# A sandwich of attention and feed-forward blocks: a stretch of products moved, a norm moved to VectorE, and the ending split over two banks

## The chip, the cores and the metric

The kernel runs on one core of one Trainium2 chip. The core has five engines that run their own instruction streams in order: TensorE (PE in the profile, its weight loads PEld), VectorE (DVE), ScalarE (ACT), GpSimd (POOL), and SyncE (SP), which here issues the DMAs. They wait for each other by semaphores. The metric is the device time of one execution in microseconds (us). Before the change it is 620.03 us, the median of 3 runs (619.95 to 620.16).

## The reference

The input x is 2 batches of 512 tokens with 256 features, in float32. Four blocks follow each other, each with a norm before and a norm after it:

```python
x = x + layernorm(L0_attn(layernorm(x)))   # 16 heads of 128, RoPE, causal softmax
x = x + layernorm(L0_ffn(layernorm(x)))    # 2048 wide, gelu(gate) * up, 4-bit weights with scales
x = x + layernorm(L1_attn(layernorm(x)))   # linear attention, running sums along the tokens
x = x + layernorm(L1_ffn(layernorm(x)))    # 688 wide, silu(gate) * up, weights looked up in a table of 16
```

The linear attention has phi(x) = elu(x) + 1 on q and k, the running sums of k and of k*v along the tokens, q*sum(k*v) / (q*sum(k) + eps), and an output product. All products are float32.

## The kernel before

The 1024 tokens are cut into units of 256 tokens (u = 0 to 3, two per batch), and a unit into two tiles of 128 tokens. NT is 4 tiles per batch, HT is 2 tiles per unit, NK is 2 chunks of 128 features.

*Start.* The four tiles of the first batch are loaded, `statistics`, `variance` and `factor` make mean and 1/deviation for each tile, and ScalarE subtracts the mean. For the first two tiles the transposed, normalised x comes out of a product with a diagonal matrix that holds 1/deviation (`diagonal(t)`, tile `wu`); that product is PE's first real work, after 18 warm-up products on constants. ScalarE writes the first two tiles through `spread(t)`, an access pattern that permutes the columns while it goes.

*First attention.* The 32 pairs of batch and head run as slots, `slot(i)` with i up to NS + 1 (NS = 32). In one slot head i's scores are made and softmaxed, head i-1's probabilities are turned and multiplied with the values (`attended(i - 1)`, `ps_t<-pT,v`), and head i-2 is projected out (`projected_out(i - 2)`). `turned_p(i)` writes four DVE transposes and the four DMAs that finish the transposed probabilities (`pT<-turned`). In the last slots the pairs of gate and up products of the first FFN unit (`main`, which is `ffn_hidden(0)`) fill PE; each `next(main)` is one product, `ps_mm<-xT,wg` or `ps_s<-xT,wu`. ScalarE makes gelu (`ge<-ps_mm`), VectorE the product with up (`hT<-ge,ps_s`), which frees the banks.

*Feed-forwards and second attention.* `ffn_hidden(u)` and `ffn_out(u)` run for the four units in turn, then `silu_hidden(u)` and `silu_out(u)`. Among their products the planner puts the rest: `linear_attention(u)`, with its projections (`ps_mm<-xT,wqkv_sb`, `ps_s<-xT,wqkv_sb`), exponentials, running sums, reciprocals and output product (`wout_sb,lT`). `norms(u, y, stage, to)` makes the norm after a block and the one ahead of the next: statistics on DVE, the power for 1/deviation on POOL, the normalised tile `ln` on ACT, its 32x32 transposes on DVE (`tr<-ln`), and four DMAs that put the blocks in place (`xT<-tr`). For the third norm of the last unit alone it goes another way: ACT writes `ln` through a permuting access pattern, PE makes four transposes (`ps_t<-ident,ln`, line 288), and ACT copies the result out.

*Order.* The order of all instructions is fixed when the program is written. A planner (`Times`, `Engine`, lines 109 to 183) keeps a clock per engine with a cost for each instruction. Each chain of small work is a generator that yields the time to wait, for example `yield until(lT)`; `poll()`, called after each product, writes the steps of the chains that are due by that clock. So a chain's step that becomes due earlier lands ahead of a later product. Engines then run their own streams in this order. Every instruction of DVE, ACT and POOL has line 183 in the profile, every DMA line 165, every product line 281.

*Banks.* Products write PSUM banks under four names, mm, s, t and o, with two banks each. A product that wants a bank waits until the reader of the one before last has finished.

*Halved products.* `halved[0]` makes `matmul` write each product as two of 64 columns of weights instead of one of 128. It is on from the attention on, and `norms` turns it off at the third norm of the last unit.

*The end.* `silu_out(3)` makes the last tile's product in two halves of 128 columns in one bank. Then `written` takes the statistics of each half (`st_last`), joins them, takes 1/deviation on POOL, subtracts the mean, multiplies and adds to x, and writes the tile out.

Of the kernel before, what the change touches and what calls it, by code (L numbers as in the profile page):

```python
# [10 lines left out]
F32 = mybir.dt.float32  # L11
# [5 lines left out]
AF = mybir.ActivationFunctionType  # L17
ALU = mybir.AluOpType

P = 128  # L20
# [13 lines left out]
HT = 2  # L34
# [156 lines left out]
def sandwich_kernel(  # L191
    ctx: ExitStack,
    tc: tile.TileContext,
    x: bass.AP,
    wq: bass.AP,
    wk: bass.AP,
# [98 lines left out]


    x0 = [const.tile([P, NT, D], F32, name=f"x0_{b}") for b in range(B)]
    cols_sb = const.tile([P, 3 * NH + 2 * NK], F32, name="cols_sb")
    for t in range(NT):
        sync.dma_start(out=x0[0][:, t, :], in_=x[0][t * P : (t + 1) * P, :])  # L300
    sync.dma_start(out=cols_sb, in_=cols)
# [51 lines left out]
    def add_scaled(x, y, rstd):  # L353

        vector.scalar_tensor_tensor(x, y, rstd, x, ALU.mult, ALU.add)

    def norms(u, y, stage, to, eps=EPS, strided=False):
# [13 lines left out]
        by_blocks = (u, stage) != (NUNIT - 1, 3)  # L371
        for j in range(HT):
            rstd, shift = second[j]
            yield until(rstd, shift)
            to_n, from_x = n[:, j, :], x[j]
            if not by_blocks:
                to_n = to_n.rearrange("p (k f c) -> p k f c", k=NK, c=4)
                from_x = from_x.rearrange(
                    "p (c f k) -> p k f c" if strided else "p (k c f) -> p k f c", k=NK, c=4
                )  # L380
            elif strided:
# [4 lines left out]
        if by_blocks:  # L386

            tr = acts.tile([P, 4, NK, HT, 32], F32, tag="ln", name=f"tr{stage}_{u}")
            for j in range(HT):
                vector.transpose(  # L390
                    tr[:, :, :, j, :], n[:, j, :].rearrange("p (k c f) -> p c k f", k=NK, c=4)
                )
            for a in range(4):
                sync.dma_start(
                    out=to[:, a].rearrange("p k j t -> p (k j t)"),
                    in_=tr[32 * a : 32 * a + 32].rearrange("f c k j t -> f c (k j t)"),
                )
        else:

            halved[0] = False  # L400
            pt = bank("t")
            for kc in range(NK):
                for j in range(HT):
                    transpose(
                        pt[:, kc * TU + j * P : kc * TU + (j + 1) * P],
                        n[:, j, kc * P : (kc + 1) * P],
                    )
            for kc in range(NK):
                scalar.copy(
                    to[:, :, kc].rearrange("p a j t -> p j a t"),  # L410
                    pt[:, kc * TU : (kc + 1) * TU].rearrange("p (j a t) -> p j a t", j=HT, a=4),
                )
# [97 lines left out]
    with ExitStack() as at:  # L510
# [69 lines left out]
        def first_norms(b, wait):  # L580
# [104 lines left out]
            else:  # L685
# [13 lines left out]
                for t in range(NT):  # L699
                    statistics(t)  # L700
                    variance(t)
                    if t < HT:
                        scalar.activation(*spread(t), AF.Identity, bias=mv[:, t, 0:1], scale=-1.0)
                    factor(t)
# [28 lines left out]
            for kc in range(NK):  # L733
# [5 lines left out]
                )  # L739
            yield 30.0  # L740
            while holder[0] is not None:
# [362 lines left out]
        def slot(i):  # L1104
# [96 lines left out]
            if i in (1, 2):  # L1201

                ahead = projection("q", i + 2)
                next(ahead)
            if 1 <= i < NS + 1:
                attended(i - 1)
# [8 lines left out]
            if i < NS - HG:  # L1215
                if i > 1:
                    values(i // 2 + 1, odd)
            elif i <= NS:
                next(main)
                next(main)  # L1220
# [58 lines left out]
    def linear_attention(u):  # L1279
# [63 lines left out]
        for ch in range(NK):  # L1343
            for t in range(HT):
# [3 lines left out]
                yield 0.3  # L1348
        yield until(lT)
        po = bank("t" if last else "o")  # L1350
# [11 lines left out]

        yield from norms(u, [po[:, j * D : (j + 1) * D] for j in range(HT)], 3, t, 16 * EPS)
        xT3[u] = t
# [8 lines left out]
    def silu_hidden(u):  # L1373
# [12 lines left out]
        for o in range(0, NO, 2):  # L1386
# [22 lines left out]
            yield  # L1409

    def silu_out(u):
        for t in range(HT):
            po = bank("o")[:, :D]
            last = (u, t) == (NUNIT - 1, HT - 1)
            for cs in [slice(0, P), slice(P, D)] if last else [slice(0, D)]:
                for o in range(NO):
                    matmul(
                        po[:, cs],
                        hT2[u % 2][:, o, t * P : (t + 1) * P],
                        wd[:, o, cs],  # L1420
                        o == 0,
                        o == NO - 1,
                    )
                    if o % 2 and (o + 1 < NO or cs.stop < D):
                        yield
            begin(written(u, t, po))
            yield

    def written(u, j, y):
# [10 lines left out]

        st = small.tile([P, 2, 6], F32, tag="st", name="st_last")
        mv = small.tile([P, 2], F32, tag="mv", name="mv_last")
        for c in range(2):
            vector.bn_stats(st[:, c, :], y[:, c * P : (c + 1) * P])
        vector.bn_aggr(mv, st)
        ve = small.tile([P, 1], F32, tag="ve", name="ve_last")
# [3 lines left out]
        centred = acts.tile([P, HT, D], F32, tag="ln", name="centred")[:, 0, :]  # L1450
        vector.tensor_scalar(centred, y, mv[:, 0:1], None, ALU.subtract)
        add_scaled(x, centred, rstd)
# [28 lines left out]
def _layout(i):  # L1481
# [21 lines left out]
    def turned(w):  # L1503
        return w.reshape(4, 32, -1).transpose(1, 0, 2).reshape(w.shape)

    def by_half(s):
        return s.reshape(4, 2, -1).transpose(1, 0, 2).reshape(s.shape)
# [12 lines left out]
    named = {  # L1520
        "x": i[a0 + "h"],
        "wq": by_head_chunk(i[a0 + "wq"]),
        "wk": by_head_chunk(i[a0 + "wk"]),
# [43 lines left out]
```

## Time and profile before

| | |
|---|---|
| median of 3 runs | 620.03 us (619.95 to 620.16) |
| the profiled execution | 620.06 us |
| its span in the profile | 618.1 us, so 1.96 us lie outside it |
| instructions | 13150 |
| PE busy | 611.0 us, 99% of the span |
| DVE busy | 483.3 us, 78% |
| ACT busy | 312.0 us, 50% |
| POOL busy | 275.9 us, 45% |
| TensorE clock granted | full in all 40 slices |

All times of a trace count from the start of the span. In a row of the timeline the first number is the start, the second the length of a run of like instructions (their number after the x), then engine, line, operation, tile written and tiles read. What stands in brackets at the end is how long the engine was idle before it, and what ended the idle time. In a row of groups the columns are line, engine, operation, tiles, shapes and count, then busy time and mean of one in ns, then idle time ahead.

### The profile page before, as it was taken

What the parts mean: (1) busy time and instruction counts of PE and PEld (TensorE: products, weight loads), DVE (VectorE), ACT (ScalarE), POOL (GpSimd) and SP (SyncE); (2) the same over time, 40 slices, a digit from 0 to 9 for tenths busy, and PEclk for the clock granted to TensorE, in tenths of its full rate; (3) what the DMA queues carried; (4) which work ended last, traced back from release to release, by engine and by line L of the source; (5) the groups of instructions that cost most, each with busy time, mean ns of one, the idle gap of its engine ahead of it and who ended that gap; (6) DMA issues with size and microseconds to landing.
All of it is one profiled execution on the core that took longest, in us unless ns stands there. A gap on an engine that the chain in (4) does not pass through costs nothing.

```text
span 618.1 us, 13150 instructions
## 1 busy us (share of the span) xinstructions
PE 611.0 (99%) x4876; PEld 397.7 (64%) x4876; DVE 483.3 (78%) x1159; ACT 312.0 (50%) x717; POOL 275.9 (45%) x353
## 2 busy tenths in 40 slices
PE   8999999999999999999999999999999999999996
PEld 6555655555555555656667788888666666666676
DVE  6989989887887999989899989779985463384853
ACT  5657776776666657667566741234123313425130
POOL 5355656454553575755667300440360160163341
PEclk9999999999999999999999999999999999999999
DMA  8467474755547547556543521310000001001000
GB/s 227 137 168 211 107 198 125 173 165 147 155 125 182 164 113 190 156 143 173 124 130 63 131 57 24 113 35 18 1 20 19 1 1 35 1 5 31 27 27 18
DMA packets 43599, 60.90 MB, mean 99 GB/s; under 512 B 5136, under 2 KB 31504, under 8 KB 43536
## 3 DMA queue, kind: packets, MB, share of 16 engines
q1 hardware_dynamic: 43536, 60.07, 37.5%
q8 instruction: 39, 0.64, 0.4%
q14 instruction: 24, 0.20, 0.1%
HBM read 28.33 MB, written 1.05 MB: 48 GB/s over the span
## 4 chain that ended last, share of the span: by engine, by line
PE 96%; DVE 2%; issue 1%; DMA 0%; POOL 0%; ACT 0%; POOLq 0%; DVEq 0%
PE ps_mm L281 39%; PE ps_o L281 22%; PE ps_s L281 21%; PE ps_t L281 14%; DVE rr L183 0%; DMA x<-in_x 0%; DVE turned L183 0%; DVE st L183 0%; DVE wu L183 0%; DVE xTv L183 0%; DVE xT L183 0%; DVE ra L183 0%; DVE hT L183 0%; POOLq L1563 0%; PE ps_t L288 0%
## 5 line engine op out<-in xcount | busy, mean ns | idle before, releaser
L183 DVE SCALAR_TENSOR_TENSOR rr<-ps_mm,cols_sb,sin_sb 64x512 f32<-64x512 f32 (+1 forms) x126 | 93.4, 741 | 3.7 <-PE ps_mm L281 0.8
L183 POOL TENSOR_TENSOR wg<-wg,scratch 128x752 f32<-128x752 f32 x30 | 53.8, 1794 | 91.0 <-DVE scratch L183 88.7
L281 PE MATMUL ps_mm<-xT,wg 128*64 128x256 f32 (+2 forms) x680 | 85.8, 379 | 0.0
L183 ACT ACTIVATE p<-p,mn 128x512 f32<-128x512 f32 (+3 forms) x128 | 70.3, 551 | 28.1 <-DVE mn L183 27.9
L281 PE MATMUL ps_s<-xT,wu 128*64 128x256 f32 (+1 forms) x652 | 82.0, 379 | 0.0
L281 PE MATMUL ps_o<-wd,hT 128*64 128x256 f32 (+2 forms) x676 | 78.3, 375 | 0.0
L281 PE MATMUL ps_t<-pT,v 128*64 128x256 f32 (+3 forms) x512 | 75.1, 433 | 0.0
L281 PEld LDWEIGHTS ps_mm<-xT,wg 128*64 128x64 f32 (+2 forms) x680 | 56.5, 139 | 19.1 <-ACT ge L183 0.3
L281 PEld LDWEIGHTS ps_o<-wd,hT 128*64 128x64 f32 (+1 forms) x676 | 55.5, 141 | 20.7
L183 ACT ACTIVATE p<-p,rs 128x512 f32<-128x512 f32 (+3 forms) x128 | 61.4, 551 | 11.4 <-DVE rs L183 9.8
L281 PEld LDWEIGHTS ps_s<-xT,wu 128*64 128x64 f32 (+1 forms) x652 | 54.4, 139 | 18.1 <-DVE hT L183 0.3
L281 PEld LDWEIGHTS ps_t<-pT,v 128*64 128x64 f32 x512 | 42.0, 137 | 34.8 <-issue 25.5
L281 PE MATMUL ps_o<-wo,oT 128*64 128x256 f32 x512 | 61.4, 379 | 0.0
L281 PE MATMUL ps_mm<-xT,wq 128*64 128x512 f32 (+2 forms) x252 | 59.4, 582 | 0.4 <-ACT xT L183 0.4
L281 PE MATMUL ps_mm<-xT,wk 128*64 128x512 f32 x248 | 59.1, 592 | 0.0
L281 PEld LDWEIGHTS ps_o<-wo,oT 128*64 128x64 f32 x512 | 42.5, 137 | 25.2 <-issue 15.1
L183 POOL TENSOR_TENSOR ra<-ra,cos_sb 128x512 f32<-128x512 f32 (+1 forms) x33 | 41.1, 1246 | 39.3 <-ACT ra L183 37.1
L281 PE MATMUL ps_s<-kT,qT 128*64 128x64 f32 (+5 forms) x384 | 57.4, 425 | 0.1
L183 DVE STREAM_TRANSPOSE turned<-p 128x512 f32<-128x512 f32 (+3 forms) x128 | 54.1, 479 | 2.1 <-DMA pT<-turned 0.6
L281 PE MATMUL ps_mm<-wv,xTv 128*64 128x256 f32 x464 | 55.6, 379 | 0.0
L183 DVE TENSOR_TENSOR hT<-ge,ps_s 128x512 f32<-128x512 f32 x32 | 21.8, 684 | 41.6 <-ACT ge L183 22.9
L281 PEld LDWEIGHTS ps_s<-kT,qT 128*64 128x64 f32 x384 | 34.3, 137 | 24.2 <-issue 7.5
(157 smaller groups left out, 933.6 us busy)
## 6 DMA issues: line engine op xcount, KB each, us to landing
pT<-turned SPq DMA_DIRECT2D x128, 208.0 KB, 3.9
wo<-in_wo SPq DMA_DIRECT2D x17, 256.0 KB, 4.1
wv<-in_wv SPq DMA_DIRECT2D x16, 256.0 KB, 4.0
wq<-in_wq SPq DMA_DIRECT2D x15, 256.0 KB, 4.4
wk<-in_wk SPq DMA_DIRECT2D x15, 256.0 KB, 4.0
xT<-tr SPq DMA_DIRECT2D x44, 64.0 KB, 2.1
pk_g<-in_gate_p SPq DMA_DIRECT2D x4, 256.0 KB, 4.3
sc_g<-in_gate_s SPq DMA_DIRECT2D x8, 128.0 KB, 4.1
```

What stands on the lines that cost most here:

```text
L183: return write(*args, **more)
L281: nc.tensor.matmul(out[part], lhsT=lhsT[:, part], rhs=rhs, start=start, stop=stop, **more)
```

## The change

It has five parts.

1. The first two tiles of x are loaded from a second copy of the input, `x_turned`, whose columns are permuted on the host. ScalarE then writes the normalised tiles without `spread`. The two tiles are loaded again in the plain order, from the plain input, 20 us of the planner's clock later, for the residual.
2. In slot NS - 2 the two `next(main)` that stood after `turned_p` stand ahead of `attended(i - 1)`, so head 29's values come after the FFN's pair of products.
3. The last unit's output product of the linear attention is due 0.8 us of the planner's clock earlier. With this and the other parts the planner places several steps differently. The projections of the linear attention: unit 0's one gate/up pair later among the products of `ffn_hidden(1)`, those of units 1 and 2 one pair earlier, unit 3's after 20 of the 24 halved products of `silu_out(0)` instead of after 8. The output products: unit 0's after all eight blocks of `ffn_out(1)` instead of within the seventh, unit 1's after six blocks of `ffn_out(2)` instead of seven, unit 2's after seven blocks of `ffn_out(3)` instead of after that and a pair of `silu_hidden(0)`, unit 3's after all 24 halved products of `silu_out(1)` instead of 20.
4. `last_norms` takes the place of `norms` for the third norm of the last unit. VectorE subtracts and multiplies in one instruction per tile and makes the transposes, and four DMAs put the blocks in place. PE's transposes, ACT's `ln` and the copies are gone, and `halved[0]` stays on to the end.
5. In `silu_out(2)` the first two of six row blocks are taken for both tiles, then the other four for both. In `silu_out(3)` the two halves of the last tile go to two banks, o and t, and the statistics of the first half stand ahead of the second half's products. The subtraction of the mean is two instructions of 128 columns instead of one.

```diff
     for t in range(NT):
-        sync.dma_start(out=x0[0][:, t, :], in_=x[0][t * P : (t + 1) * P, :])
+        src = x_turned if t < HT else x[0]
+        sync.dma_start(out=x0[0][:, t, :], in_=src[t * P : (t + 1) * P, :])
...
+    def last_norms(u, y, to, eps):
+        x = [xs[u][:, j, :] for j in range(HT)]
+        def factors(y, eps):
...
+            vector.bn_stats(st, y)
+            vector.bn_aggr(mv, st)
+            ve = small.tile([P, 1], F32, tag="ve", name="ve")
+            vector.tensor_scalar(ve, mv[:, 1:2], eps, None, ALU.add)
+            rstd = small.tile([P, 1], F32, tag="rstd", name="rstd")
+            pool.tensor_tensor(rstd, ve, mhalf[:, :1], ALU.pow)
+            return mv, rstd
+        first = [factors(t, eps) for t in y]
+        second = []
+        for j in range(HT):
+            add_scaled(x[j], y[j], first[j][1])
+            second.append(factors(x[j], EPS))
+        yield 1.0
...
+        for j in range(HT):
+            mv, rstd = second[j]
+            vector.tensor_scalar(n[:, j, :], x[j], mv[:, 0:1], rstd, ALU.subtract, ALU.mult)
+            turned_about(tr, n, j)
+        brought(to, tr)
+        yield 1.0
+        for j in range(HT):
+            mv, rstd = first[j]
+            shift = small.tile([P, 1], F32, tag="shift", name="shift")
+            pool.tensor_scalar(shift, mv[:, 0:1], rstd, -1.0, ALU.mult, ALU.mult)
+            scalar.activation(x[j], x[j], AF.Identity, bias=shift)
+        yield until(to)
...
-        else:
-            halved[0] = False
-            pt = bank("t")
-            for kc in range(NK):
-                for j in range(HT):
-                    transpose(
...
                     if t < HT:
-                        scalar.activation(*spread(t), AF.Identity, bias=mv[:, t, 0:1], scale=-1.0)
+                        scalar.activation(
+                            n[0][:, t, :],
+                            x0[b][:, t, :],
+                            AF.Identity,
+                            bias=mv[:, t, 0:1],
+                            scale=-1.0,
+                        )
...
-            yield 30.0
+            yield 20.0
+            if b == 0:
+                for t in range(HT):
+                    sync.dma_start(out=x0[b][:, t, :], in_=x_rows[b][t * P : (t + 1) * P, :])
+            yield 10.0
...
+            if i == NS - 2:
+                next(main)
+                next(main)
             if 1 <= i < NS + 1:
                 attended(i - 1)
...
-            elif i <= NS:
+            elif NS - 2 < i <= NS:
                 next(main)
                 next(main)
...
-        yield until(lT)
+        yield until(lT) - 0.8 * last
...
-        yield from norms(u, [po[:, j * D : (j + 1) * D] for j in range(HT)], 3, t, 16 * EPS)
+        y = [po[:, j * D : (j + 1) * D] for j in range(HT)]
+        yield from last_norms(u, y, t, 16 * EPS) if last else norms(u, y, 3, t, 16 * EPS)
...
     def silu_out(u):
+        halves = [slice(0, P), slice(P, D)]
+        if u == NUNIT - 2:
+            parts = [(t, slice(0, D), os) for os in (range(NO - 4), range(NO - 4, NO)) for t in range(HT)]
+        else:
+            parts = [(0, slice(0, D), range(NO))]
+            parts += [(1, cs, range(NO)) for cs in (halves if u == NUNIT - 1 else [slice(0, D)])]
+        po = {}
+        for n, (t, cs, os) in enumerate(parts):
+            if (t, cs.start) not in po:
+                po[t, cs.start] = bank("t" if cs.start else "o")[:, :D]
...
+            if cs.stop - cs.start < D:
+                if not last_st:
+                    last_st.append(small.tile([P, 2, 6], F32, tag="st", name="st_last"))
+                vector.bn_stats(last_st[0][:, len(last_po), :], po[t, cs.start][:, :P])
+                last_po.append(po[t, cs.start][:, :P])
...
-        vector.tensor_scalar(centred, y, mv[:, 0:1], None, ALU.subtract)
+        for c in range(2):
+            cs = slice(c * P, (c + 1) * P)
+            vector.tensor_scalar(centred[:, cs], last_po[c], mv[:, 0:1], None, ALU.subtract)
```

More of the change, by code (lines that the diff above doesn't have):

```diff
@@ L194, in sandwich_kernel @@
     x: bass.AP,
+    x_turned: bass.AP,
     wq: bass.AP,
@@ L294, in until @@
         return max(0.0, times.written(*aps) - now[0])
+    x_rows = x
     x0 = [const.tile([P, NT, D], F32, name=f"x0_{b}") for b in range(B)]
@@ L355, in add_scaled, with turning, turned_about, brought @@
         vector.scalar_tensor_tensor(x, y, rstd, x, ALU.mult, ALU.add)
+    def turning(u, stage):
+        return acts.tile([P, 4, NK, HT, 32], F32, tag="ln", name=f"tr{stage}_{u}")
+    def turned_about(tr, n, j):
+        vector.transpose(tr[:, :, :, j, :], n[:, j, :].rearrange("p (k c f) -> p c k f", k=NK, c=4))
+    def brought(to, tr):
+        for a in range(4):
+            sync.dma_start(
+                out=to[:, a].rearrange("p k j t -> p (k j t)"),
+                in_=tr[32 * a : 32 * a + 32].rearrange("f c k j t -> f c (k j t)"),
+            )
+    def last_norms(u, y, to, eps):
+        x = [xs[u][:, j, :] for j in range(HT)]
+        def factors(y, eps):
+            st = small.tile([P, 6], F32, tag="st", name="st")
+            mv = small.tile([P, 2], F32, tag="mv", name="mv")
+            vector.bn_stats(st, y)
[11 more added lines that the diff above has]
+        yield 1.0
+        n = acts.tile([P, HT, D], F32, tag="ln", name=f"n_{u}")
+        tr = turning(u, 3)
+        for j in range(HT):
[10 more added lines that the diff above has]
+        yield until(to)
     def norms(u, y, stage, to, eps=EPS, strided=False):
@@ L368, in norms @@
         n = acts.tile([P, HT, D], F32, tag="ln", name=f"ln{stage}_{u}")
-        by_blocks = (u, stage) != (NUNIT - 1, 3)
         for j in range(HT):
@@ L375, in norms @@
             to_n, from_x = n[:, j, :], x[j]
[L376 to L381, printed above, removed]
+            if strided:
                 to_n = to_n.rearrange("p (k m) -> p k m", k=NK)
@@ L385, in norms @@
         yield until(n)
-        if by_blocks:
-            tr = acts.tile([P, 4, NK, HT, 32], F32, tag="ln", name=f"tr{stage}_{u}")
-            for j in range(HT):
[L390 to L397, printed above, removed]
-        else:
-            halved[0] = False
-            pt = bank("t")
-            for kc in range(NK):
-                for j in range(HT):
-                    transpose(
[L405 to L412, printed above, removed]
+        tr = turning(u, stage)
+        for j in range(HT):
+            turned_about(tr, n, j)
+        brought(to, tr)
         for j in range(HT):
@@ L702, in first_norms @@
                     if t < HT:
-                        scalar.activation(*spread(t), AF.Identity, bias=mv[:, t, 0:1], scale=-1.0)
+                        scalar.activation(
[4 more added lines that the diff above has]
+                            scale=-1.0,
+                        )
                     factor(t)
@@ L1409, in silu_hidden @@
             yield
+    last_st, last_po = [], []
     def silu_out(u):
[L1412 to L1427, printed above, removed]
+        halves = [slice(0, P), slice(P, D)]
[8 more added lines that the diff above has]
+                po[t, cs.start] = bank("t" if cs.start else "o")[:, :D]
+            for o in os:
+                matmul(
+                    po[t, cs.start][:, : cs.stop - cs.start],
+                    hT2[u % 2][:, o, t * P : (t + 1) * P],
+                    wd[:, o, cs],
+                    o == 0,
+                    o == NO - 1,
+                )
+                if o % 2 and (o + 1 < NO or cs.stop < D):
+                    yield
+            if cs.stop - cs.start < D:
[3 more added lines that the diff above has]
+                last_po.append(po[t, cs.start][:, :P])
+            if o == NO - 1 and cs.stop == D:
+                begin(written(u, t, po[t, cs.start]))
+                yield
     def written(u, j, y):
@@ L1439, in written @@
             return
-        st = small.tile([P, 2, 6], F32, tag="st", name="st_last")
         mv = small.tile([P, 2], F32, tag="mv", name="mv_last")
-        for c in range(2):
-            vector.bn_stats(st[:, c, :], y[:, c * P : (c + 1) * P])
-        vector.bn_aggr(mv, st)
+        vector.bn_aggr(mv, last_st[0])
         ve = small.tile([P, 1], F32, tag="ve", name="ve_last")
@@ L1504, in turned, with turned_columns @@
         return w.reshape(4, 32, -1).transpose(1, 0, 2).reshape(w.shape)
+    def turned_columns(x):
+        return x.reshape(-1, NK, 4, 32).transpose(0, 1, 3, 2).reshape(x.shape)
     def by_half(s):
@@ L1521, in _layout @@
         "x": i[a0 + "h"],
+        "x_turned": turned_columns(i[a0 + "h"][0, : HT * P]),
         "wq": by_head_chunk(i[a0 + "wq"]),
```

## The prediction

> **What bounds the kernel now.** I read the totals and the chain first, then the 20 us windows to find where TensorE (PE) is not full, then the timeline at each of those places.
>
> ```profile
> PE 611.0 (99%) x4876; PEld 397.7 (64%) x4876; DVE 483.3 (78%) x1159; ACT 312.0 (50%) x717; POOL 275.9 (45%) x353
> PE 96%; DVE 2%; issue 1%; DMA 0%; POOL 0%; ACT 0%; POOLq 0%; DVEq 0%
> ```
>
> PE is the bound from end to end. An edit is worth time only if it removes PE work, removes a wait of PE, or shortens the start before PE has data or the end after its last product. In the windows PE holds 20.00 of 20 us nearly everywhere; 0 to 20 has 17.95, 340 to 360 has 19.92, and the last 18 us have 13.19. The start, by the timeline:
>
> ```profile
> 3.51 1.47 ACT L183 ACTIVATE n<-x,mv 128x256 f32<-128x256 f32 x2 [1.09 <-DVE mv L183]
> 4.88 0.68 ACT L183 ACTIVATE wu<-wu,rstd 128x128 f32<-128x128 f32 x2
> 5.32 1.16 PE L281 MATMUL ps_t<-wu,n 128*128 128x128 f32 x8 [0.65 <-ACT wu L183]
> ```
>
> The first real product waits for ScalarE (ACT): two strided normalisations of 0.74 us each, then the scaled diagonal. At the border between attention and the first FFN:
>
> ```profile
> 351.70 1.02 PE L281 MATMUL ps_s<-kT,qT 128*64 128x512 f32 x4
> 352.06 0.69 DVE L183 TENSOR_TENSOR hT<-ge,ps_s 128x512 f32<-128x512 f32 x1
> 352.81 0.84 PEld L281 LDWEIGHTS ps_s<-kT,qT 128*64 128x64 f32 x8 [0.54 <-DVE hT L183]
> ```
>
> The scores of the last head wait until VectorE (DVE) has read the FFN's up product out of the same pair of banks (0.54 idle on the weight loads). In the second FFN unit, after two loads of ACT's function table:
>
> ```profile
> 432.43 1.28 ACT L183 ACT_TABLE_LOAD   x1
> 433.73 1.09 ACT L183 ACTIVATE ge<-ps_mm 128x512 f32<-128x512 f32 x2
> 434.38 1.49 PEld L281 LDWEIGHTS ps_mm<-xT,wg 128*64 128x64 f32 x16 [0.34 <-ACT ge L183]
> ```
>
> Near the end, the third norm of the last unit:
>
> ```profile
> 593.34 0.83 ACT L183 ACTIVATE ln<-x,shift,rstd 128x256 f32<-128x256 f32 x1
> 594.31 0.42 PEld L288 LDWEIGHTS ps_t<-ident,ln 128*128 128x128 f32 x4 [0.38 <-ACT ln L183]
> 594.32 0.66 PE L288 MATMUL ps_t<-ident,ln 128*128 128x128 f32 x4
> 594.81 3.62 PE L281 MATMUL ps_o<-wd,hT 128*128 128x256 f32 x16
> ```
>
> Four transposes sit in PE's stream, after a short wait for ACT. And after the last product, work that nothing hides:
>
> ```profile
> 613.23 0.49 DVE L183 BATCH_NORM_STATS2 st_last<-ps_o 128x6 f32<-128x128 f32 x2
> 613.76 0.21 DVE L183 BATCH_NORM_AGGREGATE mv_last<-st_last 128x2 f32<-128x12 f32 x1
> 614.18 0.48 DVE L183 TENSOR_SCALAR centred<-ps_o,mv_last 128x256 f32<-128x256 f32 x1
> 614.24 0.55 POOL L183 TENSOR_TENSOR rstd_last<-ve_last,mhalf 128x1 f32<-128x1 f32 x1 [1.72 <-DVE ve_last L183]
> 614.83 0.48 DVE L183 SCALAR_TENSOR_TENSOR x<-centred,rstd_last,x 128x256 f32<-128x256 f32 x1 [0.16 <-POOL rstd_last L183]
> ```
>
> The sums run against the profiled execution, 620.06 us (span 618.1, 1.96 outside it), within 0.03 of the median of 620.03.
>
> **The change part by part.**
>
> *Start.* The second strided normalisation (0.74) becomes contiguous; the contiguous x<-x,shift of the same size on ACT has a mean of 0.496. The first is not what counts: the second begins when its mean is ready (4.21) and now ends at about 4.70 instead of 4.98. The first diagonal then starts some 0.25 earlier; the second is held by its rstd (POOL, 4.48 + 0.55 = 5.03), but its products come half of 1.16 us after the first ones. I take -0.24, ends 0 (a load such as wv, wanted 0.15 to 0.25 after it lands, is late next) and -0.48 (the saving on both normalisations, 2 x 0.24). The two extra loads of x, 128 KB each, cost SP two issues of 0.43 to 0.6, ahead of wk, wv, wo and the first packed gate weights. By the landings in the trace all these have microseconds to spare but one: head 1's transposed scores land about 0.44 before they are needed, and their issue (42.45) lies well after the loads. I take 0; upper end +0.5, half the added issue time.
>
> *Border.* The first gate/up pair (two products of 1.73) goes ahead of head 29's values, so its hT multiply (0.69) ends about 350.5 instead of 352.75, before the scores of 351.7 want the bank. The block from 351.70 to 354.00 takes 2.30 now; the same block without the wait takes 2.02 (14.52 to 16.54). So -0.28, ends 0 and -0.30. Behind the moved multiply stand head 30's four DVE transposes (1.69): they end at about 352.15 instead of 348.8, their four DMAs go out some 3.4 later and land by about 359; PE reads them at 362.4. Head 29's values also end 3.45 later and with them ACT's oT, whose reader comes one head later. Both covered, by 3 us or more.
>
> *Turns of the planner.* The L1 projections of unit 0, among the second FFN unit's products, come one gate/up pair later, so the exponentials and their two table loads fall beside the last pair, whose hT is first read over 5 us into the out product. The wait at 434.38 goes: the gate product's natural place is 434.29 and the out product's 437.74 against 437.95, -0.21. Those of unit 1 come one pair earlier and meet the same wait in a smaller form (+0.05, ends 0 and +0.21). Sum -0.16. The wout products only change places with products of equal banks: 0.
>
> *Last third norm.* Gone from PE: four transposes, 594.32 to 594.81, 0.49, and the wait before them, 0.10: -0.59. In their place stands a DVE chain and four DMAs. From the end of the wout product (585.58) the second statistics of the second tile now end at 589.93, so 4.35 later; add the factor (0.15 + 0.57 with hops of 0.3), the normalisation 0.53, a transpose 0.50 and part of an interleaved hT multiply: 6.7. The same four DMAs issued elsewhere have 0.60 to 0.65 between them and the last lands 4.02 after the first issue: 10.74 after the wout product. From then to hidden(3)'s first gate product PE has seven more gate or up products of 0.863 and 12 out products of 0.432 (two records of 0.216 each): 11.22. Slack 0.48, so I take the whole 0.59; ends -0.59 and, by the late transfers of rival 1, +0.37.
>
> *Planner at 560.* The last unit's projection comes 2.6 us later (after 20 of the 24 halved out products of `silu_out(0)` instead of 8). DVE's queue then holds its scans in front of a hT multiply whose bank the up product wants at 576.95; by my placement it ends at 576.91. I take 0, ends 0 and +0.35. The last unit's lT is ready near 584.4, and its product wants it at 584.72.
>
> *Halved products to the end.* The last 18 us run as pairs of 64 columns instead of 128. The rows: eight records of halves of a gate product take 0.86 (586.45 to 587.31), four whole ones, the same work, 0.87 (598.26 to 599.13). I take 0; upper end +0.65, if the weight loads of the short last products bind. The Trainium skill ("TensorE: Matmul & The Clock Gate", "Packing small matmuls") speaks against this: column tiles run side by side, but three gave 2.38 times the speed and not three. By that ratio some 18 us of products would grow by a quarter, an estimate of +4.6 us and a time near 623; by the rows it is nothing. The rows are of this kernel and this form, so the sum goes by them.
>
> *End.* With two banks the first half's statistics run while PE still works; one of the two st_last remains, -0.21. The centring in two halves (one more instruction) ends about when POOL's rstd_last does: 0 to +0.06.
>
> Sum: -0.24 - 0.28 - 0.16 - 0.59 - 0.21 = -1.48, about +0.05 for the centring: -1.43. 620.03 - 1.43 = 618.6.
>
> **Rivals.**
> 1. *The transfers take the place of the transposes.* The four DMAs of 558.69 needed 3.87 of issue in all (one took 1.97), and landed 5.46 after their transposes. With that, the landing is 12.2 after the wout product, PE waits 0.96, and the third norm costs 0.37 more than now: 619.6 (619.1 with half the lateness past the slack). For: the slack is 0.48. Against: the other nine groups are regular.
> 2. *The multiply at 577 and the loads at the start.* If PE stands 0.35 at 576.95, or the start's 0.24 is eaten by a late load, 618.85 to 618.95; both 619.2.
> 3. *Slower.* One mechanism: a late last piece of the third norm. Its worst row of xT landings is 4.6 us against a median of 2.2, 2.4 more on the last DMA: 1.9 of standing PE before hidden(3), 620.5. It decides the sign from 1.9 us of lateness (0.48 slack + 1.43). For: DVE is in order and every step of the chain is on it. Against: chain and transfers are near their medians nearly everywhere else.
> 4. *The change doesn't do what it says:* the waits at 352.8 and 434.4 only move to the next multiply; the start, the transposes and the end remain, 619.0.
>
> **How the numbers follow.** About 0.2% (1.24 us) is what a measurement of this kernel can tell from no change, so the border is 618.79 below. Forecast within 0.3 of 618.6: 0.50. Rival 1: 0.18. Rival 2: 0.14. Rival 3: 0.09. Rival 4: 0.09. The forecast's own range is 618.2 to 618.9. All bounds at their best give 618.3, and what I have not seen may add a little; with the upper ones in turn (+0.65, +0.5, rival 3) 619.5 to 620.5. Range 617.9 to 620.2. Faster: most of the forecast, a third of rival 2, little of the others: 0.52; slower: the upper part of rival 3 and what I can't see: 0.10; same: 0.38.
>
> **What would show it.** In the changed profile: the first PE product with wu at about 5.05; no idle ahead of the last head's scores, and that block 2.0 long; no wait of a gate load for ge near 434; no L288 in the last 30 us, with hidden(3)'s first gate product following the last out product at once and the last xT landing before it; eight half records in 0.86 to the end; one st_last after the last product and the end some 0.2 sooner after it. Wrong would be: PE waiting for xT<-tr near 597, a weight load waiting for hT near 577, or last products of more than 0.11 per pair.

## The result, and the profile after

The changed kernel takes 618.99 us (median of 17 executions, 618.55 to 619.35) against 620.16 us for the kernel before (17 executions beside them, 619.91 to 620.95): a ratio of 0.998, with a 95% interval of 0.9973 to 0.9986, so 1.24 us less by the ratio, 0.87 to 1.67. The profiled execution took 619.33 us (span 617.5, 1.8 outside it), so it is one of the longer ones of this kernel, while the profile of before (620.06) was one of the shorter ones of its own. The spans differ by 0.6 us only, and that has to be kept in mind when the two traces are compared.

The totals and the chain of the profile after:

```profile
PE 611.6 (99%) x4968; PEld 429.6 (70%) x4968; DVE 484.4 (78%) x1168; ACT 308.4 (50%) x713; POOL 276.1 (45%) x347
PE 99%; DVE 1%; POOL 0%; issue 0%; ACT 0%; DVEq 0%; POOLq 0%
```

PE is the bound as before. The start, PE's timeline (start, length, line, tiles):

```profile
0.98 4.21 PE L580 MATMUL ps_o<-wu 128*128 128x128 f32 x18 [0.98 <-POOL mhalf L183]
5.16 2.03 PE L282 MATMUL ps_t<-wu,n 128*128 128x128 f32 x8
7.46 1.15 PE L282 MATMUL ps_mm<-xT,wq 128*128 128x256 f32 x4 [0.27 <-ACT xT L183]
```

The first real product starts 0.16 earlier than before (5.16 against 5.32), but the same eight records take 2.03 us instead of 1.16, and the wq products start 0.55 later (7.46 against 6.91). The border between attention and FFN:

```profile
350.61 0.69 DVE L183 TENSOR_TENSOR hT<-ge,ps_s 128x512 f32<-128x512 f32 x1 [1.97 <-PE ps_s L282]
352.10 1.18 PE L282 MATMUL ps_s<-kT,qT 128*64 128x448 f32 x4
353.98 2.01 PE L282 MATMUL ps_mm<-xT,wg 128*64 128x256 f32 x16
```

The multiply now comes ahead of the scores, which begin at 351.99 and end 2.0 us later; the wait for hT is gone. At 434 us the gate product follows at 434.26, its natural place, with no wait ahead of it. But three weight loads wait where none waited before (PEld, then ACT ahead of the third):

```profile
452.16 0.63 PEld L282 LDWEIGHTS ps_o<-wout_sb,lT 128*64 128x64 f32 x8 [0.37 <-POOL lT L183]
...
482.91 1.49 PEld L282 LDWEIGHTS ps_mm<-xT,wg 128*64 128x64 f32 x16 [0.33 <-ACT ge L183]
...
556.47 0.63 PEld L282 LDWEIGHTS ps_mm<-xT,wg 128*64 128x64 f32 x8 [0.42 <-ACT si L183]
...
555.34 0.60 ACT L183 ACTIVATE ln<-x,shift,rstd 128x256 f32<-128x256 f32 x1
555.84 0.58 ACT L183 ACTIVATE si<-ps_mm 128x512 f32<-128x512 f32 x1
```

In PE's stream they cost 0.25 (the output product of unit 0 takes 1.98 from 451.53 to 453.51, without a wait 1.73), 0.09 and 0.17: 0.51 together. A fourth wait, for a hidden tile near 577 us, costs 0.02. Near the end, by engine:

```profile
592.81 5.35 PE L282 MATMUL ps_o<-wd,hT 128*64 128x256 f32 x48
597.99 1.03 PE L282 MATMUL ps_mm<-xT,wg 128*64 128x256 f32 x8
...
593.48 2.49 SPq L165 DMA_DIRECT2D xT<-tr  x4
```

hidden(3)'s first gate product follows the last out product at once: 48 records of 0.108 make 5.18, and 592.81 + 5.18 is 597.99. The four DMAs start 6.72 us after the end of the output product (586.76), the last is issued at about 595.4 and lands 2.1 later, 0.5 before it is wanted. And the end:

```profile
611.60 0.30 DVE L183 BATCH_NORM_STATS2 st_last<-ps_o 128x6 f32<-128x128 f32 x1 [0.66 <-PE ps_o L282]
612.91 0.30 DVE L183 BATCH_NORM_STATS2 st_last<-ps_t 128x6 f32<-128x128 f32 x1
613.73 0.55 POOL L183 TENSOR_TENSOR rstd_last<-ve_last,mhalf 128x1 f32<-128x1 f32 x1 [1.45 <-DVE ve_last L183]
613.94 0.34 DVE L183 TENSOR_SCALAR centred<-ps_t,mv_last 128x128 f32<-128x128 f32 x1
614.38 0.48 DVE L183 SCALAR_TENSOR_TENSOR x<-centred,rstd_last,x 128x256 f32<-128x256 f32 x1
```

One of the two statistics is off the path, and the second centring (613.94 to 614.28) ends with POOL's factor (614.28). From the start of PE's last record to the end of the span it takes 4.95 us, before 5.19.

To compare traces whose starts differ, I cut each into four stretches by PE's own records: to the 14th projection of attention (near 180 us), to the 29th (344), the border to the 30th (361), from there to the last record, and to the end. The second stretch is 164.7 in both.

| | first wq product | wq to 14th projection | border | to PE's last record | last record to end |
|---|---|---|---|---|---|
| before | 6.91 | 172.76 | 16.54 | 252.01 | 5.19 |
| after | 7.46 | 172.48 | 16.24 | 251.70 | 4.95 |

So in these two executions: start +0.55, then -0.28, border -0.30, rest -0.31, end -0.24.

### The profile page after: what moved, and what is told of

Its sections match the earlier page's. It is cut to its first block, busy times and chain, and to the rows that moved or that the text cites. A ratio compares the mean times of both kernels' runs of the same rounds, so it can differ in the third digit from the quotient of the medians.

```text
span 617.5 us, 13337 instructions
## 1 busy us (share of the span) xinstructions
PE 611.6 (99%) x4968; PEld 429.6 (70%) x4968; DVE 484.4 (78%) x1168; ACT 308.4 (50%) x713; POOL 276.1 (45%) x347
## 4 chain that ended last, share of the span: by engine, by line
PE 99%; DVE 1%; POOL 0%; issue 0%; ACT 0%; DVEq 0%; POOLq 0%
PE ps_mm L282 40%; PE ps_o L282 22%; PE ps_s L282 21%; PE ps_t L282 15%; PE ps_o L580 1%; DVE x L183 0%; DVE centred L183 0%; POOL rstd L183 0%; ACT xT L183 0%; DVE st L183 0%; PE ps_s L289 0%; DVE st_last L183 0%; POOL ve L183 0%; DVE mv_last L183 0%; DVE mv L183 0%
## 5 line engine op out<-in xcount | busy, mean ns | idle before, releaser
L282 PE MATMUL ps_mm<-xT,wg 128*64 128x256 f32 x704 | 87.3, 379 | 0.0
L282 PE MATMUL ps_s<-xT,wu 128*64 128x256 f32 x672 | 83.3, 379 | 0.0
L282 PE MATMUL ps_o<-wd,hT 128*64 128x256 f32 (+1 forms) x704 | 76.8, 375 | 0.0
L282 PEld LDWEIGHTS ps_mm<-xT,wg 128*64 128x64 f32 x704 | 60.5, 137 | 16.1 <-ACT si L183 0.4
L282 PEld LDWEIGHTS ps_o<-wd,hT 128*64 128x64 f32 x704 | 59.5, 137 | 15.5
L282 PEld LDWEIGHTS ps_s<-xT,wu 128*64 128x64 f32 x672 | 58.7, 137 | 14.6 <-DVE hT L183 0.3
L282 PEld LDWEIGHTS ps_t<-pT,v 128*64 128x64 f32 x512 | 48.0, 137 | 28.8 <-issue 21.1
L282 PEld LDWEIGHTS ps_o<-wo,oT 128*64 128x64 f32 x512 | 47.8, 137 | 20.0 <-issue 13.8
L282 PE MATMUL ps_s<-kT,qT 128*64 128x448 f32 (+5 forms) x384 | 57.2, 424 | 0.0
L183 ACT ACTIVATE ln<-x,shift,rstd 128x256 f32<-128x256 f32 x22 | 13.3, 610 | 79.6 <-POOL shift L183 43.1
```

The source lines that it names most:

```text
L183: return write(*args, **more)
L282: nc.tensor.matmul(out[part], lhsT=lhsT[:, part], rhs=rhs, start=start, stop=stop, **more)
```

## The experiments

**One part alone.** Four kernels, each the kernel before with one part of the change. First the start: `x_turned`, the contiguous normalisation and the second load.

```diff
-        sync.dma_start(out=x0[0][:, t, :], in_=x[0][t * P : (t + 1) * P, :])
+        src = x_turned if t < HT else x[0]
+        sync.dma_start(out=x0[0][:, t, :], in_=src[t * P : (t + 1) * P, :])
...
-                        scalar.activation(*spread(t), AF.Identity, bias=mv[:, t, 0:1], scale=-1.0)
+                        scalar.activation(n[0][:, t, :], x0[b][:, t, :], AF.Identity, bias=mv[:, t, 0:1], scale=-1.0)
```

> Only part 1 (two tiles of x loaded in permuted column order, ScalarE's normalisation contiguous, two extra loads). Theory A (the prediction's step): the first product starts about 0.24 us earlier and all of PE's stream with it: 0.24 us faster. Theory B (from the two traces): the first product does start earlier, by 0.15 to 0.25 us, but the gain does not reach the end: PE's speed doubles at a moment that differs from execution to execution (4.0 us in the profile of before, 6.9 us in the profile of after), and the wait for transposed probabilities at 170 us (0.19 us long in before) takes up what PE is ahead. B expects less than 0.1 us faster in the median, scattered over 0.5 us or more, and a longer wait near 170 us in the profile if the early products ran at full speed.

Measured: 620.15 us (11 executions, 619.63 to 621.06), ratio 0.9999 (0.9991 to 1.0008). ScalarE's normalisation takes 0.51 instead of 0.74, as expected, and the time is the same within 0.5 us. The profile again has slow early products:

```profile
0.98 4.21 PE L560 MATMUL ps_o<-wu 128*128 128x128 f32 x18 [0.98 <-POOL mhalf L183]
5.29 1.79 PE L282 MATMUL ps_t<-wu,n 128*128 128x128 f32 x8
7.52 1.15 PE L282 MATMUL ps_mm<-xT,wq 128*128 128x256 f32 x4 [0.43 <-ACT xT L183]
```

The second tile's statistics waited 0.25 for its load here, which took most of the gain at the first product (5.29, against 5.32 before). Next the border alone:

```diff
+            if i == NS - 2:
+                next(main)
+                next(main)
             if 1 <= i < NS + 1:
                 attended(i - 1)
...
-            elif i <= NS:
+            elif NS - 2 < i <= NS:
```

> Only part 2 (the first gate/up pair ahead of head 29's values). Theory A (the prediction's step with the planner's turns): -0.28 at the border, -0.21 at 434 us, +0.05 in the unit after: 0.44 us faster. Theory B (from the trace of after): the saving at the border is there (0.30) and the wait at 434 us goes (0.21), but the same moves bring three new waits: 0.25 us in the output product at 452 us, 0.09 at 483, and perhaps 0.17 at 556: between 0 and 0.2 us faster. If the 0.17 at 556 is missing here, it belongs to another part.

Measured: 620.40 us (11 executions), ratio 1.0002 (0.9993 to 1.0011): no gain. The border takes 16.24, the whole 0.30 less, and the stretch behind it 252.52, 0.51 more than before: the three new waits are there, at 452, 483 and 556, and PE's four transposes hold up the stream for 0.72 instead of 0.49 (595.11 to 595.83):

```profile
592.42 2.76 PE L281 MATMUL ps_o<-wd,hT 128*64 128x256 f32 x24
595.11 0.88 PE L288 MATMUL ps_t<-ident,ln 128*128 128x128 f32 x4
595.83 2.54 PE L281 MATMUL ps_o<-wd,hT 128*128 128x256 f32 x11
```

So all the moves of projections and output products of units 0 to 3 come from this one part, through the planner's clock, and what they cost here is more than what the border saves. The third norm alone (its function, the call, the product 0.8 earlier, `halved` on to the end):

```diff
-        yield until(lT)
+        yield until(lT) - 0.8 * last
...
+        yield from last_norms(u, y, t, 16 * EPS) if last else norms(u, y, 3, t, 16 * EPS)
```

> Only parts 3 and 4 (third norm of the last unit by VectorE with DMAs, halved products to the end, output product 0.8 us earlier in the planner's clock). Theory A (the prediction's step): 0.59 us faster, no wait of PE for the transfers, eight half records in 0.86 us. Rival: the transfers land after the last out product, PE waits up to 0.96 us near 597 us and the time is 0 to 0.4 us longer than before. The planner puts the output product after 16 of 24 halved products here instead of 24, so the slack of the transfers is 1.7 us longer than in after; but PE may wait for lT at the product itself, 0.1 to 0.5 us.

Measured: 620.26 us (11 executions), ratio 1.0002 (0.9994 to 1.0011). Neither theory: the transposes are gone and nothing waits for the transfers, but PE waits for a hidden tile in the middle of the out product (PE's, DVE's and ACT's timelines):

```profile
592.78 1.03 PE L281 MATMUL ps_o<-wd,hT 128*64 128x256 f32 x8
594.59 4.54 PE L281 MATMUL ps_o<-wd,hT 128*64 128x256 f32 x40 [0.77 <-DVE hT L183]
...
593.84 1.02 DVE L183 TENSOR_TENSOR hT<-si,ps_s 128x512 f32<-128x512 f32 x2 [1.60 <-ACT si L183]
...
592.42 0.91 ACT L183 ACTIVATE x<-x,shift 128x256 f32<-128x256 f32 x2 [12.64 <-POOL shift L183]
593.24 1.11 ACT L183 ACTIVATE si<-ps_mm 128x512 f32<-128x512 f32 x3
```

592.78 + 0.86 is 593.64, the product starts at 594.59: 0.95 lost, more than the 0.59 saved. ACT's silu stands behind the shift of x, which waits for POOL. The end alone (two banks; it holds the other order in `silu_out(2)` too):

```diff
+            if (t, cs.start) not in po:
+                po[t, cs.start] = bank("t" if cs.start else "o")[:, :D]
...
+                vector.bn_stats(last_st[0][:, len(last_po), :], po[t, cs.start][:, :P])
```

> Only part 5 (two banks for the last tile, statistics of the first half during the second half's products, centring in two). Theory A (the prediction's step): 0.16 to 0.21 us faster, all of it after the last product; centring ends no later than POOL's factor. Rival: the second half's statistics wait for the first's, or the two centrings end after POOL's factor: 0.1 us or less. Everything ahead of the last products as before.

Measured: 620.08 us (11 executions), ratio 0.9997 (0.9989 to 1.0006). From PE's last record to the end 5.05 against 5.19: 0.14 less, a little under the expected 0.16.

None of the four moves the time by itself, by sums of -0.1 to +0.2 us, and together they gain 1.24. So parts of the change need each other. The next kernels show which.

**The changed kernel again, and without one part.** The unchanged `after` first:

> The changed kernel once more, as the measure for the three beside it, and for the start: if the moment at which PE's products double in speed differs between executions of one kernel, this profile has its last slow product at another time than 6.8 us, its first wq product at another time than 7.46, and the whole stream from there to 170 us is moved by as much. If the change itself makes the early products slow, it is again 6.8 and 7.46.

Measured: 618.85 us (11 executions), ratio 0.998 (0.9971 to 0.9989). PE's products became fast at 4.6 us here, not at 7.0, and the wq products began at 7.28 all the same, because the second tile of x came late (DVE, PE):

```profile
4.16 0.43 DVE L183 BATCH_NORM_STATS2 st<-x 128x6 f32<-128x256 f32 x1 [0.63 <-DMA x<-in_x_turned]
...
5.69 1.16 PE L282 MATMUL ps_t<-wu,n 128*128 128x128 f32 x8 [0.73 <-ACT wu L183]
```

Behind the start the stretches are 172.55, 16.24, 251.64 and 4.95, within 0.07 of the first trace. Now without part 2, so with the border as before:

```diff
-            if i == NS - 2:
-                next(main)
-                next(main)
...
-            elif NS - 2 < i <= NS:
+            elif i <= NS:
```

> The changed kernel without part 2 (the first gate/up pair stays behind head 29's values); the planner then puts the projections and output products of units 0 to 2 where before has them. Theory A (the prediction's terms): 0.44 us slower than the changed kernel (0.28 at the border, 0.16 at the planner's turns). Theory B (from the traces and border alone): the border's 0.30 and the 0.21 at 434 us come back as waits, and the three new waits of 0.25, 0.09 and 0.17 go, so within 0.15 us of the changed kernel.

Measured: 622.87 us (5 executions, 620.95 to 623.47), ratio 1.0037 (1.0022 to 1.0051): neither theory, 4.0 us longer than with the part. The timelines of PE, DVE and ACT:

```profile
592.45 1.03 PE L282 MATMUL ps_o<-wd,hT 128*64 128x256 f32 x8
595.65 6.14 PE L282 MATMUL ps_o<-wd,hT 128*64 128x256 f32 x40 [2.17 <-DVE x L183]
...
593.52 1.02 DVE L183 TENSOR_TENSOR hT<-si,ps_s 128x512 f32<-128x512 f32 x2 [1.61 <-ACT si L183]
594.57 0.42 DVE L183 TENSOR_TENSOR hT<-si,ps_mm 48x256 f32<-48x256 f32 x1
595.02 0.48 DVE L183 SCALAR_TENSOR_TENSOR x<-ps_o,rstd,x 128x256 f32<-128x256 f32 x1
...
592.10 0.91 ACT L183 ACTIVATE x<-x,shift 128x256 f32<-128x256 f32 x2 [12.64 <-POOL shift L183]
```

PE waits 2.3 us for an out bank. The third unit's out product takes both its banks at once in its new order, and the second is still held by unit 1's second tile, whose reader on VectorE (x, 595.02) stands behind the whole third norm and behind three multiplies, held up by a wait of 1.61 for ACT. Without part 2 the planner puts unit 3's output product after 16 of unit 1's 24 halved out products, so the norm's work is written ahead of that reader; with part 2 it comes after all 24, and the reader is ahead. And after the wait the products run slowly for 3 us: 40 records take 5.96 us to the next gate product (601.61), where 40 at 0.108 would take 4.3. The windows show the granted clock as the number after the five busy times:

```profile
592.00:596.00 4.00, 1.83 (x16) 1.03 (x14) 2.28 (x5) 1.92 (x5) 0.30 (x2) 0.94 0.30 66
596.00:598.00 2.00, 2.00 (x12) 1.24 (x10) 0.00 (x0) 0.00 (x0) 0.00 (x0) 0.50 0.20 66
598.00:600.00 2.00, 2.00 (x18) 1.34 (x16) 0.00 (x0) 0.00 (x0) 0.00 (x0) 0.77 0.00 0
600.00:602.00 2.00, 2.00 (x22) 1.43 (x20) 0.79 (x3) 0.00 (x0) 0.98 (x3) 1.00 0.00 0
```

The granted clock falls to 0.50 after the idle 2.3 us and is back at 1.00 by 600. The wait itself is 2.3 and the slow products 1.65, 4.0 in all. One of the five executions took 620.95 us, 2.1 over the changed kernel, with a mean clock of 0.999: so it seems to have paid the wait and not the slow products.

The norm and the order in the third unit's out product, on the kernel before:

```diff
+        if u == NUNIT - 2:
+            for os in (range(NO - 4), range(NO - 4, NO)):
+                for t in range(HT):
+                    if t not in po:
+                        po[t] = bank("o")[:, :D]
...
```

> Parts 3 and 4 as in norm alone, and of part 5 only the order in the third unit's output product: the first two row blocks for both tiles, then the other four. Theory: the wait of 0.95 us for the hidden tile at 594.6 goes, because four products now stand ahead of the one that needs it, and the saving of the transposes is seen whole: 0.5 to 0.6 us faster than before. Rival: what norm alone lost is the chain on VectorE itself, and PE waits elsewhere (at hidden(3)'s first gate product for the transfers): 0.2 us faster or less.

Measured: 623.16 us (5 executions, 621.46 to 624.00), ratio 1.0041 (1.0026 to 1.0055). The wait for the hidden tile is gone, but the one for the bank is there (2.16 idle ahead of 595.78, then slow products), since unit 3's output product stands after 16 here too. This is the same trap by another way, and my expectation missed it.

**Holding the planner's turns.** The changed kernel with two due times moved:

```diff
+            yield (0.0, 3.6, 0.0, 0.0)[u]
             yield from linear_attention(u)
...
-        yield until(lT) - 0.8 * last
+        yield until(lT) + (0.6, 0.0, 0.0, -0.8)[u]
```

> The changed kernel with two of the planner's due times moved: unit 0's output product due 0.6 us later, so that it stands behind the next gate product, and unit 1's linear attention begun 3.6 us later, so that the projections and output products of units 1 to 3 stand where before has them. Theory B: the waits at 452 us (0.25), 483 (0.09) and 556 (0.17) all go, the savings at the border and at 434 stay: 0.4 to 0.5 us faster than the changed kernel, 618.5 us. Rival (the waits only move to other places): within 0.15 us of the changed kernel.

Measured: 622.47 us (5 executions, 620.73 to 622.72), ratio 1.0031 (1.0019 to 1.0044). The waits at 452, 483 and 556 are gone. But unit 3's output product went back to its place after 16, and the wait for the bank with the slow products is there again. So one number more was changed, unit 3's due time, from -0.8 to 0.8:

> The last kernel (turns held) with one number changed: the last unit's output product is due 1.6 us later, so it stands after all 24 halved out products of unit 1 instead of after 16. Theory: the 2.2 us wait there came from this place alone (the reader of unit 1's second out bank stood behind the whole third norm on VectorE); now the reader is ahead of it, the wait and the slow products after it are gone, and the time is 3 to 4 us shorter than turns held. The third norm's chain now starts behind that reader, 0.3 to 0.9 us later, so PE may wait 0 to 0.6 us for the transfers near 598: 618.4 to 619.1. Rival (the two orders in the third unit's out product or the norm itself make the wait): it stays above 620.5.

Measured: 618.32 us (5 executions, 618.04 to 618.77), ratio 0.9968 (0.9955 to 0.998), 4.15 us less than with -0.8 by the medians and 3.9 by the ratios. PE and SP near the end:

```profile
592.13 5.46 PE L282 MATMUL ps_o<-wd,hT 128*64 128x256 f32 x48
597.31 1.15 PE L282 MATMUL ps_mm<-xT,wg 128*64 128x256 f32 x8
...
593.00 2.49 SPq L165 DMA_DIRECT2D xT<-tr  x4
```

No wait: 592.13 + 5.18 is 597.31, and the transfers that start at 593.00 land in time. In PE's order this pair differs in the place of one product alone; with it the reader, five more steps of VectorE and one silu of ScalarE come ahead of the norm. The same turns with unit 3 exactly as in the changed kernel:

```diff
+            yield (0.0, 3.6, 0.0, 2.0)[u]
             yield from linear_attention(u)
...
-        yield until(lT) - 0.8 * last
+        yield until(lT) + (0.6, 0.0, 0.0, -0.8)[u]
```

> The changed kernel with the turns of units 0 to 2 held as in turns held, and unit 3's projections and output product where the changed kernel has them (its linear attention begun 2.0 us later), VectorE's order from there the same as the changed kernel's. Theory: the waits at 452, 483 and 556 us (0.25, 0.09, 0.17) are gone and nothing takes their place: 0.4 to 0.5 us faster than the changed kernel, about 618.4. Rival: another wait of a bank takes their place in units 1 or 2: within 0.15 us of the changed kernel.

Measured: 618.64 us (8 executions, 618.07 to 619.49), ratio 0.9974 (0.9964 to 0.9984). The stretch from the 30th projection to PE's last record is 251.30 against 251.70 (and 251.64): 0.34 to 0.40 less. At 452 us the gate product now covers the wait for lT:

```profile
451.48 2.01 PE L282 MATMUL ps_mm<-xT,wg 128*64 128x256 f32 x16
453.20 2.01 PE L282 MATMUL ps_o<-wout_sb,lT 128*64 128x256 f32 x16
454.93 2.01 PE L282 MATMUL ps_s<-xT,wu 128*64 128x256 f32 x16
```

Each starts 1.73 after the one before. The wait for a hidden tile at 577, 0.02 in the changed kernel, is 0.04 here; the prediction had named it at 576.95. By the traces, holding the turns gives back 0.34 to 0.40 of the 0.51; by the medians the two held kernels are 0.2 to 0.7 us faster than the changed kernel, and the intervals overlap its own.

**The third unit's order and the start, each taken out.** The changed kernel with the plain order in `silu_out(2)`:

```diff
-        if u == NUNIT - 2:
+        if u == NUNIT:
             parts = [(t, slice(0, D), os) for os in (range(NO - 4), range(NO - 4, NO)) for t in range(HT)]
```

> The changed kernel with the third unit's out product in the plain order (six row blocks of the first tile, then six of the second). Theory: the second pair's hidden tile is ready 1.55 us after the out product starts (594.36 against 592.81 in the changed kernel's trace), and the plain order wants it after two blocks, 0.86 us: PE waits 0.6 to 0.7 us, 619.5 to 619.6. Rival: the order is worth nothing by itself, since the multiply would come earlier when nothing stands ahead of it: within 0.15 us.

Measured: 619.56 us (11 executions), ratio 0.9987 (0.9978 to 0.9996), 0.6 to 0.7 longer than the changed kernel's two medians, as expected, but only 0.4 by the ratios (0.9987 against 0.998). The wait is for the hidden tile (PE, PEld):

```profile
593.88 4.54 PE L282 MATMUL ps_o<-wd,hT 128*64 128x256 f32 x40 [0.25 <-DVE hT L183]
...
593.88 4.08 PEld L282 LDWEIGHTS ps_o<-wd,hT 128*64 128x64 f32 x40 [0.70 <-DVE hT L183]
```

In that trace the wait is 0.42 from 593.46 to 593.88, and the stretch is 252.16, 0.46 longer, so the order is worth between 0.4 and 0.5. And the changed kernel without part 1, the exact reverse of the first diff of this section:

> The changed kernel without part 1 (x in its plain order, ScalarE strided, no second load). Everything behind it in the same order. Theory A (the prediction's term): 0.24 us slower than the changed kernel. Theory B: the first product is 0.16 to 0.2 us later and some of it is taken up before 180 us: 0.05 to 0.2 us slower in the median, with both kernels scattered over 0.7 us by the moment at which PE becomes fast.

Measured: 619.21 us (11 executions, 618.86 to 619.68), ratio 0.9981 (0.9973 to 0.999), against 0.998 twice for the changed kernel. By the ratios the part is worth 0.1 us or less, by the medians, which were not taken side by side, 0.2 to 0.4; neither can be told from nothing.

## Why the prediction was right or wrong

The direction came out as predicted. The time, 618.99, is 0.4 above the 618.6 of the forecast: inside the stated range, and just above the forecast's own (618.2 to 618.9). Two terms were right, one had the wrong sign and cancelled the border's gain, and one can't be told from zero. That the sum came out near all the same is partly luck, since about 0.3 us were gained where it has no term (see the end of this section).

- *Border, -0.28:* measured -0.30 in every trace that has the part. Right. The transposes and values behind it were covered, as said.
- *Last third norm, -0.59:* from 354 us on, the changed kernel loses 0.30 in the turns (below) and its stretch is 0.31 shorter, so the norm gave 0.6. The first DMA came 6.72 after the output product where 6.7 was predicted, and the slack was 0.5 where 0.48 was. Rival 1 did not come. Right, but the prediction took it as a saving that stands by itself. The norm alone gained nothing (0.95 of waiting for a hidden tile), and norm and order together lost 3 us (2.3 of waiting for a bank and 1.7 of slow products, less what the norm saves). It pays in full only with the order in `silu_out(2)`, worth 0.4 to 0.5, and with unit 3's output product after unit 1's last out product, which one pair of kernels shows to be worth about 4 (4.15 by the medians, 3.9 by the ratios). The prediction left the first out altogether.
- *Planner's turns, -0.16:* this is the step that failed. The wait at 434 went, -0.21, as predicted, and the one in unit 1 came with 0.09 (0.05 taken, 0.21 the bound). But "The wout products only change places with products of equal banks: 0" looked at banks and not at what the product reads: unit 0's output product came ahead of its lT and waits 0.25. Nor did the step look at what unit 2's output product, coming earlier with the norm behind it, does to ACT's queue: 0.17 at 556, where silu stands behind `ln`. The term was +0.30 (0.51 less 0.21), and it eats the border's whole gain, which border alone shows in the time. Holding the turns gives most of it back (0.34 to 0.40 us).
- *Start, -0.24:* the normalisation shrank as said (0.74 to 0.51). In five of the eight profiles that have the part the first product starts at 5.08 to 5.16, near the 5.05 predicted, against 5.29 to 5.38 in the six without it. In the other three it starts at 5.29, 5.33 and 5.69, where VectorE's statistics waited 0.18 to 0.63 for the second tile of x: a late load took the gain there, though not the load that the term named. The sum also took for granted that a lead of the first product is a lead of the stream. From the first product to the wq products it takes 1.59 us where the early products are fast by then and up to 2.31 where they become fast later. And some of a lead is lost at 170 us, where PE already waited for transposed probabilities in the profile of before: with the wq products at 6.91 the stretch to the 14th projection takes 172.76, at 7.46 it takes 172.48. At the 14th projection no lead can be seen: it starts at 179.49 to 180.01 with the part and at 179.61 to 180.26 without. The term's bounds held (0 to -0.48), the value taken was too good by an amount that these runs don't settle.
- *Halved products, 0:* right. 48 records took 5.18, and no loss shows to the end. The Trainium skill's figure for column tiles ("TensorE: Matmul & The Clock Gate", "Packing small matmuls") would, by the prediction's estimate, have made the last 18 us 4.6 longer; these rows, two tiles of 64 columns in float32, have none of it.
- *End, -0.16:* 0.24 in the changed kernel, 0.14 alone. Of the 0.24, only 0.12 lies between PE's last record and the last multiply (1.91 before, 1.79 after; 1.78 in tail alone), and that is what the part was meant to save. The other 0.12 lies behind that multiply (3.28 before, 3.16 after) and is not the part's: norm alone, with the old ending, has 3.10 there, and tail alone 3.27. Right in mechanism, a little too good in size.
- *Rival 4* said that waits may only move to the next multiply and gave 619.0. It named neither place nor cause, but that is nearest to what happened: the waits at 352.8 and 434.4 went, and others of the same sum came.

By the traces the terms behind the start are -0.30, +0.30, -0.6 and -0.24: -0.84. The medians differ by 1.17. Of the rest, 0.17 lies outside the traced span: the median of an execution's time less its span is 1.94 to 1.96 us for the kernel before and 1.77 to 1.78 for the changed kernel (norm alone 1.77, border alone 1.82, tail alone 1.93, start alone 1.99). With the 0.12 behind the last multiply that makes 0.29 us for which the prediction had no term, and no run shows why it went. What is left, 0.16, lies in the start and the 170 us, where executions of one kernel differ by more than that, so I can't place it.

## What to carry to other kernels

Where a planner writes the order, an edit that moves one product also moves the planner's clock, and so the places of steps hundreds of us later; compare the written orders of the two kernels, and for each step that moved ask what it reads, what holds its bank, and whose reader now stands behind it in a queue that is served in order. Parts that gain nothing one by one may need each other: try a part both alone and taken out. A wait of more than 2 us on a busy TensorE should be priced with the slow products that may follow it.

## What the runs showed of the hardware

PE's first products run at half speed (0.213 us from one 128x128 record to the next), and they become fast (0.111) at a moment that the kernel does not set: at 4.0 us in the profile of before, 7.0 in that of after, 4.6 in the second one of after, 5.0 to 7.2 in the others, though PE starts at 0.98 in each. The windows print a granted clock of 1.00 there, but the clock's record in the trace begins only at that moment, so it is the spacing of the records that shows the slow start. How much of the difference between executions of one kernel comes from it is not shown. The Trainium skill ("TensorE: Matmul & The Clock Gate", "What's actually happening") describes a free-running window of about 3.4 us after which the clock opens. The traces agree: in all 14 the time between two recorded changes of the clock is a whole number of 3.413 us (1, 6, or 173 to 180 of them), and the moments above lie within 3.2 us of each other.

The same page asks for an idle window of about 3.4 us before the clock falls back. Here 2.3 us of waiting in a busy stream were enough in three kernels to bring the granted clock to 0.5, for 3.41 us by the clock's record, at a price of 1.65 us, and not in every execution: 11 of their 15 have a mean clock of 0.996 or 0.997, the other four of 0.999 or 1.00. The measurement decides: a shorter wait can cost the clock.
